# Quantized inner values turned by a DMA, together with another order of loads and set-up

## The chip, the cores and the metric

The kernel runs on one core of a Trainium2 chip. The core has TensorE (PE: matrix products and transposes, results in PSUM), VectorE (DVE), ScalarE (ACT), GpSimd (POOL), SyncE (SP, which only issues DMAs and waits) and 16 DMA engines. Every engine takes its own instructions in order; between engines there are only semaphores. The metric is the device time of one execution in microseconds (us).

## The reference

There are 8 sequences of 512 tokens with 256 channels. Each one goes through these steps:

```python
y = x @ W[subject].T + b[subject]              # a weight chosen by the batch's id
q, k, v = silu(y@Wq), silu(y@Wk), y@Wv         # 16 heads of 16 channels
q, k = [t*cos, t*sin]                          # positions, 32 channels a head
out = (tril(q @ k.T) @ v) @ Wo * sigmoid(y@G1@G2)
x = x + layernorm(out)
# cond2: a recurrent mixing of x
ctx = ema(x);  wg = sigmoid([x, ctx] @ Wg.T + bg);  gated = x*wg
mod = 0.5 + sigmoid(gelu(x@Wn1.T + bn1) @ Wn2.T + bn2)      # 8 traces
traces_d = ema_d(gated * mod_d)                # 8 decays, one for each trace
temporal = sum_d softmax(blend)_d * traces_d
c = layernorm((gelu(x@Wsoma.T + bsoma) * sigmoid(temporal@Wtemp.T + btemp)) @ Wout.T)
# feed-forward with quantized activations (to 127 steps) and weights (-1, 0, 1)
h = silu(quant(c) @ wq(w_gate).T) * (quant(c) @ wq(w_up).T)     # 1024 inner values
x = x + quant(h) @ wq(w_down).T
```

`quant` scales each token's row by its largest absolute value, rounds and scales back; `wq` does so with the mean absolute value of the whole weight.

## The kernel before, in words

A batch is one sequence of 512 tokens, handled as four tiles of 128 tokens. It goes through three generators: `attention(b)`, `cond2(b)` and `ffn(b)`. Two more, `setup_cond2` and `setup_ffn`, prepare constants. A planner at the end of the kernel (from L898) runs them in turn. Each generator issues some instructions, adds their estimated TensorE time to the planner's clock with `spent(work, then)`, and yields the time `then` microseconds on at which its next part is due. Of the parts that are due, the one of the lowest rank goes first: set-up (0), feed-forward (1), cond2 (2), attention (3); if none is due, the clock jumps to the earliest. This makes the program's order. The framework then assigns buffers and semaphores and orders each engine's instructions, where some move ahead of their place in the program. Attention of a batch starts once the one before has issued its second `output`; so in the middle attention(b+2), cond2(b+1) and ffn(b) run beside each other.

The feed-forward works by token tiles. `hidden(t)` (L843) multiplies the turned input `cqT` with `w_gateT` and `w_upT` (L851), takes silu on ScalarE (L854) and the product on VectorE (L855, `h`), finds each row's largest value (`hmax`, L857), and rounds to whole numbers in bf16: `hq`, 128 tokens x 1024 inner values (L861, L863). The product with `w_downT` needs the inner values on the partitions. So TensorE turns `hq` in eight blocks of 128x128 into a PSUM bank (`phq`, L875), ScalarE copies them to `hqT` (L877), and eight matmuls make `pd` (L881). VectorE scales it and adds the residual (`res`, L883), and SyncE writes the tile out (L884). The planner gives the turning 0.6 of TensorE time and makes `pd` due 1.2 later. `hidden(t+1)` is issued before tile t is turned; `h`, `hq`, `hqT` and `res` have two buffers each.

The attention turns its input (`pxT`, L212; ScalarE copies it to `xT`, L213), multiplies by the chosen weight `wt` (`py`, L219), adds `beta_a` to the residual on GpSimd (L222), and then for each token tile projects (`pkq`, `pv`, `sg`), multiplies by cosine and sine on GpSimd (`ktok`, `qtok`, L256), turns (`pkT`, `pqT`) and gathers chunk states (`pst`, `total`, `st`). `energies` and `output` follow, and at the end the gate and the layer norm (`og`, `rstd_a`, L454 to L464). The result is what cond2 turns first (`px2T`, L660). cond2 ends with its layer norm and the quantized `cq` (L795 to L817).

The beginning: SyncE loads the first input, weight and bias. ScalarE issues thirteen loads (L125 to L145 and the rows of `setup_cond2`), GpSimd the others: the weights of cond2, the small vectors, `blend` broadcast to all partitions, and the feed-forward weights, which pass through the two buffers of `h`, so that one weight is loaded after the one before has been quantized (L630). `setup_cond2` computes the softmax of `blend` on all partitions (L600 to L606), spreads its rows to `bw_r` by 16 small DMAs on SyncE (L613), and spreads the decay rates `nsp_d` to `nsp_r` by 8 small DMAs on GpSimd (L585).

Of the kernel before, what the change touches and what calls it, by code (L numbers as in the profile page):

```python
# [8 lines left out]
F32 = mybir.dt.float32  # L9
BF = mybir.dt.bfloat16  # L10
# [8 lines left out]
MAGIC = 12582912.0  # L19

# [10 lines left out]
def adaln_attn_ffn_kernel(ctx: ExitStack, tc: tile.TileContext, a: dict, out: bass.AP):  # L31
# [85 lines left out]
    def load_w(name, src, pool=cp, tag=None, eng=nc.scalar):  # L117
        rows, cols = src.shape
        t = pool.tile([P, rows // P, cols], F32, tag=tag or name, name=name)
        eng.dma_start(t, src.rearrange("(k p) n -> p k n", p=P))  # L120
        return t

    def load_row(name, src):
        t = cp.tile([P, src.shape[0]], F32, name=name)
        nc.scalar.dma_start(t, src.partition_broadcast(P))  # L125
        return t
# [7 lines left out]
    wv = load_w("wv", a["wv"])  # L134
# [4 lines left out]
    nc.scalar.dma_start(g1[:, :, :HD], a["g1"].rearrange("(k p) n -> p k n", p=P))  # L139
    g2 = cp.tile([64, C], F32, name="g2")  # L140
    nc.vector.memset(g2, 0.0)
    for u in range(2):
        nc.scalar.dma_start(g2[32 * u : 32 * u + HD, :], a["g2"])
    gamma_a = load_row("gamma_a", a["gamma_a"])
    beta_a = load_row("beta_a", a["beta_a"])  # L145

# [59 lines left out]
    def attention(b, xs, wt, bt):  # L206
# [14 lines left out]

        nc.gpsimd.tensor_add(xs, xs, beta_a.unsqueeze(1).to_broadcast([P, NT, C]))  # L222
# [179 lines left out]
        turned(3)  # L402
        spent(2.0, 0)
# [67 lines left out]
    w = {}  # L471

    def setup_cond2():

        for n in ("wgT", "wn1T", "wsomaT", "wtempT", "woutT"):
            w[n] = load_w(n, a[n], eng=nc.gpsimd)

        means = p1.tile([P, KC], F32, tag="means", name="means")
        nc.vector.tensor_reduce(means, w["woutT"], AX.X, ALU.add)
        nc.vector.tensor_scalar(means, means, 1.0 / C, None, ALU.mult)  # L480
        for k in range(KC):
            nc.vector.tensor_scalar(w["woutT"][:, k, :], w["woutT"][:, k, :], means[:, k : k + 1], None, ALU.subtract)
        for n in ("bg", "gamma_c", "beta_c"):
            w[n] = load_row(n, a[n])

        w["wn2"] = cp.tile([HN + 1, D], F32, name="wn2")
        nc.gpsimd.dma_start(w["wn2"][:HN, :], a["wn2T"])
        nc.gpsimd.dma_start(w["wn2"][HN : HN + 1, :], a["bn2"].rearrange("(o d) -> o d", o=1))
        w["bn1"] = cp.tile([HN, 1], F32, name="bn1")
        nc.gpsimd.dma_start(w["bn1"], a["bn1"].rearrange("(p o) -> p o", o=1))  # L490
        for n in ("bsoma", "btemp"):
            w[n] = cp.tile([P, KC], F32, name=n)
            nc.gpsimd.dma_start(w[n], a[n])
        yield now[0] + 6.0
        nc.vector.tensor_scalar(w["btemp"], w["btemp"], 0.5, None, ALU.mult)


        tau = p1.tile([P, D + 1], F32, tag="tau", name="tau")
        nc.gpsimd.dma_start(tau, a["taus"].partition_broadcast(P))
        tau_d = p1.tile([D, 1], F32, tag="tau_d", name="tau_d")  # L500
        nc.gpsimd.dma_start(tau_d, a["taus"][:D].rearrange("(p o) -> p o", o=1))
        sps = []
        for t, name in ((tau, "sp"), (tau_d, "sp_d")):
            e = p1.tile(list(t.shape), F32, tag=name + "_e", name=name + "_e")
            nc.vector.scalar_tensor_tensor(e, t, -1.0, t, ALU.mult, ALU.max)
            nc.scalar.activation(e, e, AF.Exp, scale=-1.0)
            sps.append(e)
        for e in sps:
            nc.scalar.activation(e, e, AF.Ln, bias=1.0)
        for t, e in zip((tau, tau_d), sps):  # L510
            nc.vector.scalar_tensor_tensor(e, t, 0.0, e, ALU.max, ALU.add)
        sp, sp_d = sps
# [483 lines left out]
```

## Time and profile before

| What | us |
|---|---|
| Median of 3 runs (lowest to highest) | 832.13 (831.72 to 835.56) |
| Profiled execution, its own time | 831.28 |
| Its span, from the first to the last instruction | 829.5 |
| TensorE busy in the span | 724.8 |
| VectorE busy | 531.7 |
| ScalarE busy | 306.0 |
| GpSimd busy | 239.8 |
| First `px2T` (cond2 of batch 0 starts) | 89.04 |
| Last `res` | 826.19 |

The profile page tells the busy time of each engine (1), the span in 40 slices (2), the DMA queues (3), the chain of waits that ended last (4), the costliest groups of instructions (5) and the DMA issues (6). In a line of the timeline, the first number is the start in us, the second the duration (of all instructions that were merged, if it ends in a count), and the bracket the idle time of the engine just before it, with what ended it. A releaser is inferred. `PEld` is TensorE's weight load, which runs beside `PE`.

### The profile page before, as it was taken

How to read it: one execution, taken by the hardware profiler on the slowest of the kernel's cores; microseconds unless marked ns; L12 is line 12 of the kernel's file. 1: busy time of each engine (PE TensorE's matmuls, PEld its weight loads, DVE VectorE, ACT ScalarE, POOL GpSimd, SP SyncE). 2: the span in 40 equal slices, each digit the busy share in tenths (PEclk: the TensorE clock that was granted, in tenths of full speed). 3: DMA queues.
4: the chain of work that ended last, by engine and by line, in shares of the span. 5: the costliest groups of instructions: out<-in, count | busy, mean ns of one | idle time of the engine just before them, and what ended most of it. 6: DMA issues, size and time to landing. Idle time of an engine off the chain costs nothing.

```text
span 829.5 us, 21857 instructions
## 1 busy us (share of the span) xinstructions
PE 724.8 (87%) x9630; PEld 496.4 (60%) x9630; DVE 531.7 (64%) x1035; ACT 306.0 (37%) x536; POOL 239.8 (29%) x274
## 2 busy tenths in 40 slices
PE   3878899989997999999997999799998998696745
PEld 2557568556773667656873777566774676464423
DVE  5897545767458755784568754776469554775375
ACT  1741432345224432373224432354226421351122
POOL 6770442311502152223522151213403250111000
PEclk8956999989998999999998999999999999897667
DMA  8411000001000010001000010000000000000000
GB/s 265 141 30 55 13 1 4 15 0 31 24 3 13 14 39 3 15 14 40 3 2 13 20 34 4 13 7 21 3 2 8 19 4 3 0 12 15 1 0 26
DMA packets 16849, 19.29 MB, mean 23 GB/s; under 512 B 3331, under 2 KB 15395, under 8 KB 16755
## 3 DMA queue, kind: packets, MB, share of 16 engines
q1 hardware_dynamic: 12418, 10.56, 4.1%
q0 software_dynamic: 2048, 5.58, 2.1%
q10 hardware_dynamic: 2288, 1.76, 0.7%
q8 instruction: 75, 1.23, 0.6%
q14 instruction: 20, 0.16, 0.1%
HBM read 13.63 MB, written 4.19 MB: 21 GB/s over the span
## 4 chain that ended last, share of the span: by engine, by line
PE 64%; DVE 20%; issue 5%; POOL 5%; DMA 3%; ACT 2%; ACTq 0%; POOLq 0%; DVEq 0%
PE ptr L749 9%; PE pwg L699 7%; PE pkq L233 5%; PE pe L313 4%; PE po L335 4%; PE ptg L766 4%; PE pw_gateT L851 3%; PE pso L678 3%; PE pd L881 3%; PE pw_upT L851 3%; PE pv L238 2%; PE pst L276 2%; PE pkT L263 2%; PE pqT L263 2%; PE phq L875 2%
## 5 line engine op out<-in xcount | busy, mean ns | idle before, releaser
L754 DVE SCALAR_TENSOR_TENSOR tempT<-ptr,bw_c,tempT 128x512 f32<-128x512 f32 x128 | 96.0, 750 | 85.6 <-PE ptr L749 83.0
L749 PE MATMUL ptr<-dm,gated 64*128 64x128 f32 x1024 | 82.8, 301 | 10.4 <-DVE tempT L754 10.4
L256 POOL TENSOR_TENSOR ktok<-sg,cs 128x512 f32<-128x512 f32 x32 | 43.6, 1363 | 153.8 <-ACT sg L240 151.7
L749 PEld LDWEIGHTS ptr<-dm,gated 64*128 64x128 f32 x1024 | 69.0, 200 | 29.1 <-issue 20.7
L233 PE MATMUL pkq<-wkq,yT 128*128 128x512 f32 x128 | 64.2, 621 | 0.2 <-ACT kT L264 0.2
L855 DVE SCALAR_TENSOR_TENSOR h<-pw_upT,steps,sig 128x512 f32<-128x512 f32 x64 | 45.8, 744 | 18.6 <-ACT sig L854 10.3
L854 ACT ACTIVATE sig<-pw_gateT,steps 128x512 f32<-128x512 f32 x64 | 42.2, 685 | 26.8 <-PE pw_gateT L851 18.0
L287 POOL TENSOR_TENSOR st<-total,own 128x256 f32<-128x256 f32 x56 | 40.8, 746 | 37.2 <-DVE total L297 37.1
L318 DVE TENSOR_TENSOR et<-pe,causal 128x512 f32<-128x512 f32 x64 | 41.1, 684 | 15.1 <-PE pe L313 15.1
L256 POOL TENSOR_TENSOR qtok<-sg,cs 128x512 f32<-128x512 f32 x32 | 43.6, 1362 | 13.7 <-PE pst L276 13.5
L851 PEld LDWEIGHTS <-cqT 128*128 128x128 bf16 x256 | 28.0, 109 | 31.7 <-issue 11.9
L851 PE MATMUL pw_gateT<-w_gateT,cqT 128*128 128x512 bf16 x128 | 45.2, 433 | 0.0
L313 PE MATMUL pe<-qT,kT 32*64 32x64 f32 x2048 | 43.3, 229 | 0.2 <-ACT sg L240 0.2
L313 PEld LDWEIGHTS pe<-qT,kT 32*64 32x64 f32 x2048 | 37.1, 141 | 9.7 <-issue 7.5
L851 PE MATMUL pw_upT<-w_upT,cqT 128*128 128x512 bf16 x128 | 42.5, 417 | 0.0
L738 POOL TENSOR_TENSOR dm<-decay,mod 128x512 f32<-128x512 f32 x32 | 33.6, 1062 | 27.3 <-PE ptr L749 27.1
L240 ACT ACTIVATE sg<-pkq 128x512 f32<-128x512 f32 x32 | 19.1, 598 | 57.6 <-PE pkq L233 57.5
L877 ACT COPY hqT<-phq 128x1024 bf16<-128x1024 bf16 x32 | 32.4, 1011 | 21.4 <-PE phq L875 21.4
L881 PE MATMUL pd<-w_downT,hqT 128*128 128x256 bf16 x256 | 35.0, 282 | 5.6 <-ACT hqT L877 5.6
L857 DVE TENSOR_REDUCE hmax<-h 128x1 f32<-128x1024 f32 x32 | 38.9, 1217 | 0.6
L219 PE MATMUL py<-xT,wt 128*128 128x512 f32 x64 | 31.3, 629 | 8.1 <-ACT xT L213 8.1
L222 POOL TENSOR_TENSOR x<-x,beta_a 128x1024 f32<-128x1024 f32 x8 | 18.9, 2368 | 66.8 <-PE pxT L212 60.1
(221 smaller groups left out, 1459.1 us busy)
## 6 DMA issues: line engine op xcount, KB each, us to landing
x<-in_x_dram SPq DMA_DIRECT2D x8, 512.0 KB
out_dram<-res SPq DMA_DIRECT2D x32, 128.0 KB
wt<-in_weightT_dram SPq DMA_DIRECT2D x8, 256.0 KB
w_gateT_raw<-in_w_gateT_dram POOLq DMA_DIRECT2D x2, 512.0 KB, 5.1
bw<-in_blend_dram POOLq DMA_DIRECT2D x2, 512.0 KB, 4.8
w_upT_raw<-in_w_upT_dram POOLq DMA_DIRECT2D x2, 512.0 KB, 3.7
w_downT_raw<-in_w_downT_dram POOLq DMA_DIRECT2D x2, 512.0 KB, 4.7
wgT<-in_wgT_dram POOLq DMA_DIRECT2D x1, 512.0 KB, 7.1
```

Of the source, the lines that this page charges most:

```text
L233: nc.tensor.matmul(pkq, yT[:, k, chunk(t)], wkq[:, k].rearrange("p e c -> p (e c)"), start=k == 0, stop=k == KC - 1)
L256: nc.gpsimd.tensor_mul(tok.rearrange("p (h e d) -> p h e d", e=2, d=HD), sgs[t][:, i].unsqueeze(2).to_broadcast([P, H, 2, HD]), cs[:, t, : ...
L287: nc.gpsimd.tensor_mul(sts[c], total[0].rearrange("p (g f) -> p g f", g=NG).unsqueeze(2).to_broadcast([P, NG, 2, 2 * HD]), own.rearrange(" ...
L313: nc.tensor.matmul(pes[e][64 * r : 64 * (r + 1), g, u, :], kT[rows, g, at], qT[rows, g, at], start=True, stop=True)
L318: nc.vector.tensor_mul(et.rearrange("p g u n -> p (g u) n"), pes[e].rearrange("p g u n -> p (g u) n"), causal.unsqueeze(1).to_broadcast([P ...
L699: nc.tensor.matmul(pwg[:, u, :], src[:, k % KC, chunk(t + u)], w["wgT"][:, k, :], start=k == 0, stop=k == 2 * KC - 1,)
L749: nc.tensor.matmul(ptr[:, r, :, t, :], gated[rows, t, chunk(k)], dm[rows, t], start=True, stop=True)
L754: nc.vector.scalar_tensor_tensor(acc, ptr[:, :, e].rearrange("p r t n -> p r (t n)"), w["bw_c"][:, k, d + e : d + e + 1], acc, ALU.mult, A ...
L851: nc.tensor.matmul(pm, cqT[:, k, chunk(t)], w[n][:, k, cols], start=k == 0, stop=k == KC - 1)
L854: nc.scalar.activation(sig, pgu[0], AF.Silu, scale=steps[:, 0, t : t + 1])
L855: nc.vector.scalar_tensor_tensor(h[:, cols], pgu[1], steps[:, 1, t : t + 1], sig, ALU.mult, ALU.mult)
L881: nc.tensor.matmul(pd, hqT[:, chunk(k)], w["w_downT"][:, k, :], start=k == 0, stop=k == KI - 1)
```

## The change

Three things are different.

*The feed-forward's turning.* One DMA with `transpose=True`, issued on SyncE's queue, takes `hq` (128x1024, bf16, in SBUF) to `hqT` (128 partitions x 8 blocks x 128). The eight TensorE transposes, the PSUM bank and ScalarE's copy are gone. The planner counts no TensorE time for it and makes `pd` due 4.0 later.

*Loads.* ScalarE issues four loads (`theta_c`, `wk`, `wq`, `wv`). All others are issued on SyncE at the start, behind the first input, and GpSimd issues none. Both halves of all three feed-forward weights have tiles of their own, which later serve as `h`, `cT`, `gated`, `c2` and `og`. `blend` is loaded once, as 8 rows.

*Set-up and small moves.* The softmax of `blend` is taken on its turned form (128 channels x 2 x 8) and spread by two TensorE transposes; the decay rates are selected by a comparison with each partition's trace number. No DMA is left in the set-up generators. They are due at 12.0 and 18.0 on the planner's clock instead of 5.0 and 5.0. The row means of `woutT` are subtracted at the end of `setup_cond2`. `h1` is a constant tile whose row of ones is written once, not in each batch. The addition of `beta_a` moves from behind `py` to behind `turned(3)`.

```diff
-    def load_w(name, src, pool=cp, tag=None, eng=nc.scalar):
+    def load_w(name, src, eng=nc.sync):
...
-        nc.scalar.dma_start(t, src.partition_broadcast(P))
+        nc.sync.dma_start(t, src.partition_broadcast(P))
...
-    wv = load_w("wv", a["wv"])
+    wv = load_w("wv", a["wv"], eng=nc.scalar)
...
+    tau = p1.tile([P, D + 1], F32, tag="tau", name="tau")
+    nc.sync.dma_start(tau, a["taus"].partition_broadcast(P))
+    blend = p1.tile([D, C], F32, tag="blend", name="blend")
+    nc.sync.dma_start(blend, a["blend"])
+    raws = {}
+
+    def load_raw(n, *places):
+        rows, cols = a[n].shape
+        half = rows // P // 2
+        raws[n] = [
+            pool.tile([P, half * cols], F32, tag=tag, name=f"{n}_raw_{s}") for s, (pool, tag) in enumerate(places)
+        ]
+        for s, raw in enumerate(raws[n]):
+            nc.sync.dma_start(
+                raw.rearrange("p (k n) -> p k n", k=half), a[n].rearrange("(s k p) n -> s p k n", p=P, s=2)[s]
+            )
+
+    load_raw("w_gateT", (p2, "h"), (p2, "h"))
+    for n in ("wgT", "wn1T", "wsomaT"):
+        w[n] = load_w(n, a[n])
+    load_raw("w_upT", (p1, "cT"), (p1, "gated"))
...
+    load_raw("w_downT", (p1, "c2"), (p1, "og"))
+    for n in ("wtempT", "woutT"):
+        w[n] = load_w(n, a[n])
...
             nc.scalar.activation(yT[:, o, :], py, AF.Identity, bias=bt[:, o : o + 1])
-
-        nc.gpsimd.tensor_add(xs, xs, beta_a.unsqueeze(1).to_broadcast([P, NT, C]))
         wt_free[0] = b + 1
...
         output(0)
         turned(3)
+
+        nc.gpsimd.tensor_add(xs, xs, beta_a.unsqueeze(1).to_broadcast([P, NT, C]))
...
+    h1 = cp.tile([HN + 1, T], F32, name="h1")
+    nc.gpsimd.memset(h1[HN : HN + 1, :], 1.0)
...
-        nsp_r = p1.tile([P, 1], F32, tag="nsp_r", name="nsp_r")
-        nc.vector.memset(nsp_r, 0.0)
-        for t in range(NT):
-            for r in range(2):
-                q = 32 * t + D * r
-                nc.gpsimd.dma_start(nsp_r[q : q + D, :], nsp_d)
+        nc.vector.tensor_mul(own_trace, own_trace, nsp[:, :D])
+        nsp_r = p1.tile([P, 1], F32, tag="nsp_r", name="nsp_r")
+        nc.vector.tensor_reduce(nsp_r, own_trace, AX.X, ALU.add)
...
-            bw = p1.tile([P, D, P], F32, tag=("gated", "c2")[k], name=f"bw_{k}")
-            nc.gpsimd.dma_start(bw, a["blend"][:, chunk(k)].partition_broadcast(P))
...
-            for t in range(NT):
-                for r in range(2):
-                    q = 32 * t + D * r
-                    nc.sync.dma_start(w["bw_r"][q : q + D, chunk(k)], bw[0:1])
+            nc.tensor.transpose(ptb[:, chunk(k)], many[:, k].rearrange("p m d -> p (m d)"), ident)
+        nc.vector.tensor_copy(w["bw_r"], ptb[:, :C])
...
-            for s in range(2):
-                raw = p2.tile([P, half * cols], F32, tag="h", name=f"{n}_raw_{s}")
-                nc.gpsimd.dma_start(raw.rearrange("p (k n) -> p k n", k=half), src[s])
+            for s, raw in enumerate(raws[n]):
                 nc.vector.tensor_reduce(sums[:, s : s + 1], raw, AX.X, ALU.add, apply_absolute_value=True)
...
-            pt = bank(f"phq_{b}_{t}", BF)
-            for k in range(KI):
-                nc.tensor.transpose(pt[:, chunk(k)], hq[:, chunk(k)], ident_bf)
-            hqT = p2.tile([P, INNER], BF, tag="hqT", name=f"hqT_{b}_{t}")
-            nc.scalar.copy(hqT, pt)
-            yield spent(0.6, 1.2)
+            hqT = p2.tile([P, KI, P], BF, tag="hqT", name=f"hqT_{b}_{t}")
+            nc.sync.dma_start(hqT, hq, transpose=True)
+            yield spent(0.0, 4.0)
             pd = bank(f"pd_{b}_{t}")[:, :C]
             for k in range(KI):
-                nc.tensor.matmul(pd, hqT[:, chunk(k)], w["w_downT"][:, k, :], start=k == 0, stop=k == KI - 1)
+                nc.tensor.matmul(pd, hqT[:, k, :], w["w_downT"][:, k, :], start=k == 0, stop=k == KI - 1)
...
-    start((0, 0), 0, "setup_cond2", setup_cond2(), 5.0)
-    start((0, 1), 0, "setup_ffn", setup_ffn(), 5.0)
+    start((0, 0), 0, "setup_cond2", setup_cond2(), 12.0)
+    start((0, 1), 0, "setup_ffn", setup_ffn(), 18.0)
```

## The prediction

> **What bounds the kernel now.** I read the first page for the engines, the chain that ended last for who carries the end, the table of stretches for where TensorE stands still, and then the timeline and the groups of the places that the change touches. On the page, TensorE is the busiest engine and has most of the chain:
>
> ```profile
> PE 724.8 (87%) x9630; PEld 496.4 (60%) x9630; DVE 531.7 (64%) x1035; ACT 306.0 (37%) x536; POOL 239.8 (29%) x274
> ...
> PE 64%; DVE 20%; issue 5%; POOL 5%; DMA 3%; ACT 2%; ACTq 0%; POOLq 0%; DVEq 0%
> ```
>
> The stretches (microseconds, then busy time of PE, PEld, DVE, ACT, POOL, the granted clock, DMA share, GB/s) tell the stages apart:
>
> ```profile
> 40.00:60.00 20.00, 12.37 (x235) 10.11 (x242) 18.12 (x20) 8.76 (x15) 16.34 (x20) 0.59 0.15 48
> 60.00:89.00 29.00, 25.44 (x501) 19.11 (x489) 22.02 (x46) 5.68 (x12) 6.07 (x6) 0.69 0.14 40
> ...
> 168.50:260.00 91.50, 84.20 (x1197) 58.35 (x1195) 57.59 (x115) 35.07 (x62) 23.05 (x26) 0.97 0.06 16
> ...
> 783.00:829.50 46.50, 25.31 (x120) 13.55 (x120) 26.86 (x58) 13.31 (x23) 1.80 (x4) 0.73 0.03 11
> ```
>
> A batch in the middle takes 91.5 us with 84.2 of TensorE. Until 89 us only the first attention and the set-up run, TensorE waits a lot, and its clock is 0.59 to 0.69. From 783 us on only the last feed-forward is left, and its chain of waits counts.
>
> The beginning, in order of time:
>
> ```profile
> 13.86 0.54 ACTq L125 DMA_DIRECT2D beta_c<-in_beta_c_dram  x1
> ...
> 16.36 5.38 PE L219 MATMUL py<-xT,wt 128*128 128x512 f32 x8 [7.35 <-ACT xT L213]
> ...
> 38.94 3.85 POOL L585 DMA_DIRECT2D nsp_r<-nsp_d  x7 [0.38 <-DVE nsp_d L516]
> ...
> 47.63 1.12 PE L263 MATMUL pkT<-ident,ktok 128*128 128x128 f32 x4 [8.16 <-DVE red L604]
> ```
>
> ScalarE issues loads until 14.40 and so copies the turned input only from 15.72, though TensorE had turned it by 9.00. TensorE then idles 8.16 us before 47.63: the ktok that it waits for is queued on GpSimd behind the nsp_r copies, the decay product and w_upT.
>
> The part that is exchanged, by groups (busy, mean ns of one, idle before and its releaser):
>
> ```profile
> L877 ACT COPY hqT<-phq 128x1024 bf16<-128x1024 bf16 x32 | 32.4, 1011 | 21.4 <-PE phq L875 21.4
> ...
> L881 PE MATMUL pd<-w_downT,hqT 128*128 128x256 bf16 x256 | 35.0, 282 | 5.6 <-ACT hqT L877 5.6
> ...
> L875 PE MATMUL phq<-ident_bf,hq 128*128 128x128 bf16 x256 | 20.5, 225 | 12.6 <-DVE hmax L824 6.0 <-DVE hq L863 5.5 <-DVE res L883 0.8
> ```
>
> One turn costs TensorE 20.5/32 = 0.64 us busy and ScalarE 1.01 us.
>
> **The change part by part.** The sum is made against the profiled execution: span 829.5, its own time 831.3 us, which is 0.85 under the median of 832.13.
>
> *Loads and set-up.* ScalarE issues four loads in place of thirteen (the last, wv, ends at 2.82), so the input's copies follow the turning at 9.00 and py starts near 10.1, not 16.36: 6.3 us off the path, if wt has landed (wv, issued nearby, landed at 9.42). GpSimd loses twenty DMA issues of 0.55 to 1.3 us and the eight nsp_r copies (4.4 us); VectorE loses the blend's broadcast arithmetic (L600 3.8, L601 2.8, L603 3.8, L604 1.9, L605 0.5, L606 3.4: 16.2 us), for which come small instructions of 0.15 to 0.2 us each, about 5 us together. Of the 8.16 us stall I take 6 away. The feed-forward weights, all in their own tiles, no longer wait for one another (GpSimd waited 8.3 us for w_upT's quantizing before it loaded w_downT, and TensorE 2.0 us at 75.44 for w_downT's sums); with the second half of the blend gone from VectorE I put the stalls between 56 and 76 us at 4.7 less. Together 17.0. The lower bound is 6.3, if the rest comes back as VectorE work in another order. The upper is 25: py at 10, some 45 us for one attention's TensorE work (busy time of its groups, an eighth each: 43.6), and 9 for the layer norm behind it give 64 instead of 89. What moves to SyncE is 27 issues of 0.4 to 0.6 us, ahead of the second batch's input; 6.8 MB at the 265 GB/s of the first slice are 26 us, and that input is read only at 82.9, which covers it. If they came late, VectorE would stand in front of them, as it did 6.1 us for woutT at 20.35.
>
> *The addition of beta_a.* It is 2.35 us of GpSimd, today at the seam of two batches:
>
> ```profile
> 250.59 2.35 POOL L222 TENSOR_TENSOR x<-x,beta_a 128x1024 f32<-128x1024 f32 x1
> 250.90 0.16 DVE L826 RECIPROCAL c_inv<-amax 128x2 f32<-128x2 f32 x1
> 250.98 1.98 DVE L808 TENSOR_TENSOR steps<-amax,wstep 128x4 f32<-128x4 f32 x1
> ```
>
> L808 has a median of 0.143 us; here it lasted until the addition was over. At the six seams some VectorE instruction is stretched so: by 1.5, 1.8, 1.2, 1.5, 1.8 and 0.7 us, 8.5 together, in front of cq or the next batch's px2T, for which TensorE waits. After turned(3) there is other TensorE work, and GpSimd is 25% busy; I credit 7 and keep 0 to 8.5.
>
> *h1's memset.* 0.52 us on GpSimd a batch, with 15.1 us idle before it and nobody waiting: nothing. If GpSimd were full it would be 0.5 a batch.
>
> *The turns off TensorE and ScalarE.* In seven feed-forwards (28 turns) other stages run beside them: 28 x 0.64 = 17.9 us of TensorE work. Of that I take the chain's TensorE share, 64%: 11.5. The bounds are 0 (VectorE sets the feed-forward's pace) and 17.9. ScalarE's 1.01 us copies lie beside TensorE's work; what TensorE waited for them (5.6) goes.
>
> *The turn by DMA.* No row shows one. Its time L, from hq to hqT in place: lowest, SyncE's issue of an SBUF-to-SBUF copy (bw_r, 0.62 us) and the landing of the tiny nsp_r copies (1.7): 2.3. Highest, eight 128x128 blocks one after another at the pace of the bw_r issues (17.71/16 = 1.11 each) and that landing: 10.6. Nearest is a transfer of the same 256 KB:
>
> ```profile
> woutT<-in_woutT_dram POOLq DMA_DIRECT2D x1, 256.0 KB, 3.1
> ```
>
> wtempT took 3.2; so 3.2 + 0.6 = 3.8 us. The planner now puts pd 4.0 us of other work behind the turn, where copy and turn had 1.8. With hq on time, 3.8 is covered. Where hq is late (TensorE stood 12.6 us for it at phq), the wait moves on to pd: no change. Without that cover each us of L costs 28 us. On SyncE a turn waits for hq, and behind it wait the outputs; ahead of it is the output of the tile before, which waits for res. SyncE stood 426 us waiting for res, so the 32 issues (20 us) are hidden, as are later inputs, which are loaded a batch ahead.
>
> The Trainium skill speaks against this step: "VectorE: DVE Perf Modes", sections "The three transpose paths" and "Rules for kernel authors", gives 1309 ns for a 128x128 bf16 block by DMA against 390 ns by TensorE, and advises TensorE when PSUM will do. By that page, block after block, L would be 10.5, an estimate, and the sum about 1,010 us. The same skill, "Advanced Engine Details and Errata", section "X-Bar Transpose (TRN2)", calls such DMAs as fast as ordinary ones, which would leave the sum as it is. No run so far shows either.
>
> *The last feed-forward* has nothing beside it. From hq to hqT it took 805.84 to 807.99 and, at the end, 822.0 to 824.2: 2.2 us; now 3.8, so 1.6 more at the last tile. Before it, turn t+1 on SyncE stands behind output t, so it starts 0.5 us after res(t) at the earliest, and res(t) is itself later: I add 3.4 over three tiles. Together 5 (bounds 1 and 4 x 8.4 = 34 at L = 10.6).
>
> Sum: 831.3 - 17.0 - 7.0 - 11.5 + 5.0 = 800.8, and 0.85 more to stand against the median: 802.
>
> **The rivals.**
> *The turn is too slow, and pd's wait takes the place of phq's.* TensorE takes its work in order, so every us beyond 4.0 stops it 28 times and the tail four times. The gains less the tail are 30.5, used up at L = 4.9. At 5.5 the time is 802 + 42 + 7 = 851; with eight blocks in a row (8.9) 802 + 137 + 20 = 959. For it speak that no row shows such a DMA and that hq is often late; against it the 3.1 for 256 KB. Chance 0.22, of which 0.09 is the block-after-block case, the one of the skill's first page.
> *TensorE does less, but the period stays*, set by VectorE's 57.6 us and the seams: 802 + 11.5 = 813. *The beginning gives only ScalarE's 6.3 us*: 802 + 10.7 = 813 too. Chance of one of them 0.18; both, 824, 0.06.
> *More than forecast*: L near 2.3, so that TensorE also loses part of the 12.6 us, and 25 at the beginning: 786. Chance 0.10.
> *Gains and a turn slightly over 4.9 cancel*: within 0.5% (828 to 836, about what a measurement of this kernel can tell from no change). Chance 0.06.
>
> **How the numbers follow.** My forecast, 795 to 808, has 0.38. Faster: 0.38 + 0.18 + 0.06 + 0.10 = 0.72; same 0.06; slower 0.22. The range leaves out about 0.07 below 785 and 0.12 above 862 (L of 5.9).
>
> **What would show it.** py near 10 us; the first px2T near 72, not 89; no 8 us TensorE stall at 40 to 48; L808 at 0.14 throughout. phq and its copy gone; pd's idle time in the middle not above some 18 us (now 12.6 + 5.6 with phq's); hq to pd in the last feed-forward 3.8 us. If pd idles 30 us or more, L is over 5 and the first rival is right; if px2T begins after 82, the beginning is mis-sized.

## The result, and the profile after

The changed kernel takes 809.15 us (median of 4 runs, 804.65 to 811.26) against 831.99 (831.72 to 835.56) before: a ratio of 0.9715 with a 95% interval of 0.9678 to 0.9752, so 21 to 27 us less. The profiled execution is the slowest of the four: its own time is 811.26 us, its span 809.6, and before had 831.28 and 829.5.

The first `px2T` of each batch cuts the span into comparable pieces. (The start of batch 1's is used, because from there on the seams of all batches look alike.)

| Piece, us | before | after | difference |
|---|---|---|---|
| start to batch 0's first `px2T` | 89.04 | 80.67 | -8.4 |
| start to batch 1's first `px2T` | 168.53 | 164.03 | -4.5 |
| from there to batch 7's, six batches | 552.0 | 537.1 | -14.9 |
| from there to the end | 109.0 | 108.5 | -0.5 |
| span | 829.5 | 809.6 | -19.9 |

From the page of after, the busy time of the engines, the chain that ended last, the group of `pd`, the group of `pcq`, and the DMA issue of the turn:

```profile
PE 696.3 (86%) x9362; PEld 473.7 (59%) x9362; DVE 517.7 (64%) x1031; ACT 269.7 (33%) x496; POOL 218.4 (27%) x238
...
PE 60%; DVE 13%; issue 3%; POOL 3%; DMA 2%; ACT 0%; POOLq 0%; DVEq 0%; ACTq 0%; SPq 0%
...
L877 PE MATMUL pd<-w_downT,hqT 128*128 128x256 bf16 x256 | 36.6, 291 | 15.9 <-DMA hqT<-hq 14.9
...
L835 PE MATMUL pcq<-ident_bf,cq 128*128 128x128 bf16 x64 | 8.2, 270 | 36.7 <-DVE cq L816 36.7
...
hqT<-hq SPq DMA_TRANSPOSE x32, 3.1
```

TensorE lost 28.5 us of work and ScalarE 36.3. The turn lands 3.1 us after its issue. `phq` is gone with its 12.6 us of idle time, and `pd` idles 15.9 in place of 5.6. `pcq`, the turning of cond2's quantized result, idles 36.7 instead of 25.3: more of TensorE's time at the seam of two batches is spent waiting for VectorE's `cq`.

TensorE's waits in the six batches in the middle (line, releaser, us in total, times, longest) tell where; first before, then after:

```profile
PE pcq L836 <- DVE cq L817: 16.0, 8, 5.7
...
PE px2T L660 <- DVE x L464: 3.8, 2, 1.9
...
PE px2T L660 <- DVE h L855: 1.7, 1, 1.7
```

```profile
PE pcq L835 <- DVE cq L816: 27.5, 12, 5.7
...
PE pd L877 <- DMA hqT<-hq: 0.2, 1, 0.2
```

So `pcq` has the longest wait there in both. With `px2T`, which directly follows it at the seam and no longer waits in after, the seams cost 21.5 us of waiting before and 27.5 after.

The waits only change places, though: the 6.2 us in front of `phq` and the 5.5 in front of `px2T` are gone, `pcq` has 11.5 more, and in all TensorE stands idle for 40.4 us of these six batches before and 41.1 after. What became less is its busy time, from 511.6 to 496.0 us.

`pd` waits 0.2 us there for the DMA in 24 turns. Most of its wait is in the last feed-forward, as its timeline shows:

```profile
784.37 3.01 SPq L873 DMA_TRANSPOSE hqT<-hq  x2
...
787.45 1.89 PE L877 MATMUL pd<-w_downT,hqT 128*128 128x256 bf16 x8 [6.81 <-DMA hqT<-hq]
...
799.65 3.00 SPq L873 DMA_TRANSPOSE hqT<-hq  x2
...
802.78 3.66 PE L877 MATMUL pd<-w_downT,hqT 128*128 128x256 bf16 x16 [7.09 <-DMA hqT<-hq]
```

The framework issues two turns behind each other (`x2`), so the last feed-forward has two such waits and not four. From the end of `hq` (799.58) to `pd` it is 3.2 us.

The beginning went otherwise than forecast. The stretches of after (columns as in the prediction):

```profile
40.00:60.00 20.00, 17.15 (x593) 13.78 (x592) 18.61 (x33) 9.41 (x22) 10.57 (x9) 1.00 0.02 4
60.00:80.70 20.70, 10.55 (x179) 7.51 (x179) 10.17 (x25) 3.10 (x6) 3.76 (x3) 0.90 0.06 15
164.00:252.70 88.70, 83.69 (x1172) 57.54 (x1170) 60.42 (x117) 31.94 (x59) 26.12 (x27) 0.96 0.12 28
```

Between 40 and 60 us TensorE now works 17.15 us of 20 (12.37 before), at a granted clock of 1.00 instead of 0.59: the stall of 8.16 us is gone. But from 60 us to the first `px2T` it works only half of the time. The timeline of that beginning in after:

```profile
14.19 0.38 PE L566 MATMUL pt_bw<-ident,blend 8*128 8x8 f32 x2 [5.97 <-DMA blend<-in_blend_dram]
...
15.77 0.21 ACT L577 ACTIVATE nsp<-nsp 128x9 f32<-128x9 f32 x1 [11.69 <-DVE nsp L576]
...
17.41 1.06 ACT L254 COPY xT<-pxT 128x512 f32<-128x512 f32 x2
...
69.24 0.16 DVE L641 TENSOR_SCALAR wstep<-pwsum 128x1 f32<-128x1 f32 x1 [9.10 <-PE pwsum L638]
...
69.63 2.87 DVE L647 TENSOR_SCALAR w_downT_raw<-w_downT_raw,winv 128x1024 f32<-128x1024 f32 x2
...
75.01 0.76 DVE L495 SCALAR_TENSOR_TENSOR og<-gate,pw 128x256 f32<-128x256 f32 x2
...
80.67 1.21 PE L661 MATMUL px2T<-ident,x 128*128 128x128 f32 x4 [7.87 <-DVE x L505]
```

ScalarE's copy of the turned input stands behind the softplus of the decay rates (`nsp`), which waits for a small load (`tau`) queued behind `x`, `wt` and others on SyncE. `py` starts at 18.02, later than before's 16.36. At the other end, VectorE stands 9.10 us for the weight sums of `w_downT`, quantizes it from 69.63 on, and only then starts `og`. (VectorE had summed the raw weights up by 45.0, but TensorE adds these sums up, `pwsum`, only at 68.70, behind `pw` and `pxT`.) A reason can be seen in the code: the second half of `w_downT`'s raw values lies in the buffer that `og` takes next.

### The profile page after: what moved, and what is told of

It is laid out like the page before. It is cut to its first block, busy times and chain, and to the rows that moved or that the text cites. A ratio compares the mean times of both kernels' runs of the same rounds, so it can differ in the third digit from the quotient of the medians.

```text
span 809.6 us, 21287 instructions
## 1 busy us (share of the span) xinstructions
PE 696.3 (86%) x9362; PEld 473.7 (59%) x9362; DVE 517.7 (64%) x1031; ACT 269.7 (33%) x496; POOL 218.4 (27%) x238
## 3 DMA queue, kind: packets, MB, share of 16 engines
q1 hardware_dynamic: 51140, 24.40, 12.5%
## 4 chain that ended last, share of the span: by engine, by line
PE 60%; DVE 13%; issue 3%; POOL 3%; DMA 2%; ACT 0%; POOLq 0%; DVEq 0%; ACTq 0%; SPq 0%
PE ptr L748 8%; PE pwg L698 6%; PE pw_gateT L850 4%; PE pd L877 4%; PE po L374 4%; PE pw_upT L850 4%; PE pe L352 3%; PE pso L677 3%; PE ptg L765 3%; PE pw L490 3%; PE pkq L272 3%; DVE c L800 2%; DMA hqT<-hq 2%; PE pst L315 2%; PE pqT L302 2%
## 5 line engine op out<-in xcount | busy, mean ns | idle before, releaser
L748 PE MATMUL ptr<-dm,gated 64*128 64x128 f32 x1024 | 79.8, 299 | 10.4 <-DVE tempT L753 10.4
L748 PEld LDWEIGHTS ptr<-dm,gated 64*128 64x128 f32 x1024 | 67.2, 200 | 25.2 <-issue 20.6
L272 PE MATMUL pkq<-wkq,yT 128*128 128x512 f32 x128 | 66.1, 634 | 0.0
L854 DVE SCALAR_TENSOR_TENSOR h<-pw_upT,steps,sig 128x512 f32<-128x512 f32 x64 | 46.1, 742 | 17.6 <-ACT sig L853 11.1
L326 POOL TENSOR_TENSOR st<-total,own 128x256 f32<-128x256 f32 x56 | 41.7, 762 | 41.1 <-DVE total L336 41.1
L877 PE MATMUL pd<-w_downT,hqT 128*128 128x256 bf16 x256 | 36.6, 291 | 15.9 <-DMA hqT<-hq 14.9
L357 DVE TENSOR_TENSOR et<-pe,causal 128x512 f32<-128x512 f32 x64 | 41.1, 684 | 13.2 <-PE pe L352 13.2
L850 PE MATMUL pw_upT<-w_upT,cqT 128*128 128x512 bf16 x128 | 44.7, 436 | 0.0
L877 PEld LDWEIGHTS <-hqT 128*128 128x128 bf16 x256 | 25.7, 104 | 27.2 <-DMA hqT<-hq 20.2
L352 PE MATMUL pe<-qT,kT 32*64 32x64 f32 x2048 | 40.1, 220 | 1.0 <-DVE et L357 1.0
L835 PE MATMUL pcq<-ident_bf,cq 128*128 128x128 bf16 x64 | 8.2, 270 | 36.7 <-DVE cq L816 36.7
L352 PEld LDWEIGHTS pe<-qT,kT 32*64 32x64 f32 x2048 | 34.4, 133 | 9.1 <-issue 7.1
L374 PE MATMUL po<-et,vz 64*32 64x64 f32 x2048 | 27.5, 225 | 14.1 <-issue 12.6
```

The lines of the kernel that those rows point to most:

```text
L272: nc.tensor.matmul(pkq, yT[:, k, chunk(t)], wkq[:, k].rearrange("p e c -> p (e c)"), start=k == 0, stop=k == KC - 1)
L326: nc.gpsimd.tensor_mul(sts[c], total[0].rearrange("p (g f) -> p g f", g=NG).unsqueeze(2).to_broadcast([P, NG, 2, 2 * HD]), own.rearrange(" ...
L352: nc.tensor.matmul(pes[e][64 * r : 64 * (r + 1), g, u, :], kT[rows, g, at], qT[rows, g, at], start=True, stop=True)
L374: nc.tensor.matmul(po[r][q : q + 32, half, u, :], *factors, start=(r, q) not in begun, stop=last)
L748: nc.tensor.matmul(ptr[:, r, :, t, :], gated[rows, t, chunk(k)], dm[rows, t], start=True, stop=True)
L850: nc.tensor.matmul(pm, cqT[:, k, chunk(t)], w[n][:, k, cols], start=k == 0, stop=k == KC - 1)
```

## The experiments

Each kernel is one edit of the changed kernel, unless it says otherwise. The table has them all; ratios are to runs of the kernel before beside them, and the pieces are those of the table above, each from one profile (before: 168.5, 552.0, 109.0). The kernel before had medians of 830.47 beside the first four kernels, 836.25 beside "w_downT elsewhere", "both of these", "no addition" and "turned twice", and 833.82 beside the others, so the ratios compare better than the times.

| Kernel | us, median (range) | ratio [95%] | to batch 1 | six batches | rest |
|---|---|---|---|---|---|
| after, again | 808.09 (803.51 to 809.70) | 0.9721 [0.9687, 0.9755] | 162.1 | 536.5 | 108.6 |
| turn on TensorE | 823.34 (821.07 to 830.79) | 0.9942 [0.9909, 0.9974] | 162.3 | 549.5 | 107.4 |
| DMA turn alone | 815.40 (812.97 to 817.16) | 0.9813 [0.9782, 0.9844] | 169.0 | 538.7 | 106.7 |
| tau first | 806.63 (803.71 to 815.71) | 0.9732 [0.9683, 0.9781] | 162.4 | 536.4 | 107.1 |
| w_downT elsewhere | 803.62 (800.56 to 806.76) | 0.9630 [0.9559, 0.9701] | 155.6 | 535.5 | 107.8 |
| both of these | 805.54 (802.77 to 807.35) | 0.9630 [0.9568, 0.9692] | 160.0 | 537.3 | 108.4 |
| no addition | 794.75 (792.24 to 797.62) | 0.9522 [0.9455, 0.9589] | 161.1 | 521.7 | 107.9 |
| addition later | 798.30 (793.36 to 800.76) | 0.9561 [0.9526, 0.9595] | 164.4 | 525.5 | 107.7 |
| turned twice | 848.41 (845.85 to 851.88) | 1.0156 [1.0085, 1.0227] | 163.1 | 565.1 | 118.9 |
| eight blocks | 996.78 (993.44 to 1003.11) | 1.1944 [1.1902, 1.1985] | 166.2 | 675.7 | 159.5 |
| pd due at once | 889.12 (885.34 to 890.91) | 1.0673 [1.0636, 1.0710] | 165.0 | 598.6 | 120.1 |
| best parts together | 792.66 (784.87 to 793.93) | 0.9487 [0.9449, 0.9526] | 155.7 | 528.5 | 106.7 |

### Which part of the change gives how much

The kernel once more, as the base of the others:

> The changed kernel once more, beside the others on the same chip. 804 to 811 us, as in its four runs; the middle six batches take 537 us between the first turnings of their x2, TensorE idles 7.9 us before the first px2T, and pd waits for the turn by DMA almost only in the last feed-forward.

Measured: 808.09. The beginning varies by 2 us between the two profiles (164.0 and 162.1 to batch 1), the six batches by 0.6.

The new beginning with the old turning:

```diff
-            hqT = p2.tile([P, KI, P], BF, tag="hqT", name=f"hqT_{b}_{t}")
-            nc.sync.dma_start(hqT, hq, transpose=True)
-            yield spent(0.0, 4.0)
+            pt = bank(f"phq_{b}_{t}", BF)
+            for k in range(KI):
+                nc.tensor.transpose(pt[:, chunk(k)], hq[:, chunk(k)], ident_bf)
+            hqT = p2.tile([P, INNER], BF, tag="hqT", name=f"hqT_{b}_{t}")
+            nc.scalar.copy(hqT, pt)
+            yield spent(0.6, 1.2)
...
```

> The new loads and set-up alone: the turn is back on TensorE and ScalarE with its old due times. Theory (the turn's 0.64 us of TensorE work a tile is what shortened the middle by 14.9 us; the new beginning gave only 4.5): about 825 us, the middle six batches again near 550. Rival A (the middle became shorter by the other moves, the turn is worth nothing): 809, middle near 537. Rival B (the new beginning is worth the predicted 17 and the turn loses): below 805.

Measured: 823.34, a ratio of 0.9942, which is 4.8 us less than before (2 to 8). To batch 1 it is as fast as after (162.3), the six batches take 549.5, 13.0 more than the 536.5 of "after, again", and the rest 107.4, 1.2 less.

The reverse, the old beginning with the DMA, its 4.0 and the new form of `hqT` put into the kernel before:

```diff
-            pt = bank(f"phq_{b}_{t}", BF)
...
-            yield spent(0.6, 1.2)
...
+            nc.sync.dma_start(hqT, hq, transpose=True)
+            yield spent(0.0, 4.0)
...
```

> The turn by DMA alone, in the kernel before with its old loads and set-up. Theory: 832 - 15 in the middle and -0.5 at the end, 816 to 818 us, with the first px2T still at 89. Rival A (the turn is worth nothing without the new set-up): 830 to 833. Rival B (only what was predicted, 11.5 less 5 of the end): 825.

Measured: 815.40, a ratio of 0.9813: 15.5 us less than before (13 to 18), 13.3 of them in the six batches. The two ratios multiplied give 0.976 against the 0.972 of both together: the parts add up. The turning by DMA carries two thirds to four fifths of the gain (15.5 of 23.2 us here, 18.4 by what is missing without it). In both comparisons the six batches show the same as above: TensorE stands idle for 40.3 us with its own turning and 40.4 in "after, again", for 40.4 in before and 39.9 with the DMA turn alone, while its busy time falls by 13.1 and by 12.8 us.

### What the beginning still waits for

`tau` and `blend` ahead of the large weights, on ScalarE's queue:

```diff
     # right behind theta_c's load
...
+    nc.scalar.dma_start(tau, a["taus"].partition_broadcast(P))
...
+    nc.scalar.dma_start(blend, a["blend"])
...
-    nc.sync.dma_start(tau, a["taus"].partition_broadcast(P))
...
-    nc.sync.dma_start(blend, a["blend"])
```

> In the changed kernel the loads of tau and blend go to ScalarE's queue right behind theta_c, ahead of wk, wq and wv. Theory (ScalarE's copy of the turned input stood behind the softplus of tau, which landed at 15.0 us; so py began at 18.0): py begins at 10 to 12, and the first px2T comes 5 to 7 us earlier, at 74 to 76; the time falls by 5 to 7 against the changed kernel. Rival (VectorE's og waits for the quantizing of w_downT, whose raw half lies in og's buffer, and this sets the end of the first attention): py earlier, px2T at 78 to 80, and the time less than 2 us lower.

Measured: `py` starts at 14.38 and not 18.02, but batch 0's first `px2T` gets no earlier: it comes at 81.02, after the same 7.87 us. That is nearer to the rival than to the theory. In this kernel's timeline VectorE stands behind `w_downT` as in after:

```profile
69.36 0.16 DVE L641 TENSOR_SCALAR wstep<-pwsum 128x1 f32<-128x1 f32 x1 [7.66 <-PE pwsum L638]
```

The other suspect is the buffer. The second half of `w_downT` goes into the tile that later serves as `soma`, which cond2 of batch 0 needs only behind `px2T`:

```diff
-    load_raw("w_downT", (p1, "c2"), (p1, "og"))
...
     # behind the second activation that makes the cosines
+    load_raw("w_downT", (p1, "c2"), (p1, "soma"))
```

> In the changed kernel the second raw half of w_downT lies in soma's buffer, not in og's, and w_downT is loaded last (behind the cosines, which hold soma until then). Theory (og could not be written before w_downT's second half was quantized, and this sets the end of the first attention): og starts with pw, VectorE's 7.7 us wait for pwsum ahead of it is gone, TensorE's 7.9 us before the first px2T go to about 1, px2T at 73 to 75 and the time 6 to 7 us under the changed kernel: 801 to 802. Rival (the quantizing is only postponed and stops something else, or the later loads come too late): px2T earlier, but the second px2T still at 162, no gain.

Measured: 803.62 us, a ratio of 0.963 against 0.972. In its timeline `og` runs first, and `w_downT` behind it:

```profile
65.84 0.75 DVE L496 SCALAR_TENSOR_TENSOR og<-gate,pw 128x256 f32<-128x256 f32 x2 [1.60 <-PE pw L491]
...
74.35 0.15 DVE L642 TENSOR_SCALAR wstep<-pwsum 128x1 f32<-128x1 f32 x1
```

```profile
73.30 1.12 PE L662 MATMUL px2T<-ident,x 128*128 128x128 f32 x3 [1.03 <-DVE x L506]
```

`px2T` starts 7.4 us earlier than in after, and its 7.87 us of waiting are down to 1.6 in two waits. At batch 1, 6.5 us of it are kept (155.6 against 162.1). So the shared buffer set the end of the first attention, and `tau` did not. (The edit also loads `w_downT` later, but VectorE takes its sums at the same time in both kernels, from 42.6 and 42.7 us on, so the load is not what lets `og` run first.) The two ratios alone do not show the gain, since their intervals overlap; it is read from the pieces, and the kernel with the best parts has it again (155.7).

Both edits at once:

> Both mends of the beginning: tau and blend loaded first, and w_downT's half out of og's buffer. Theory: with og free the 3.5 us by which py came earlier in e3_tau_first now reach the end of the first attention: px2T at 70 to 71, 9 to 10 us under the changed kernel, 798 to 799. Rival (the middle of the first attention waits for VectorE's set-up work, so an earlier py is worth nothing): like e4_down_elsewhere.

Measured: 805.54, and `px2T` at 77.23, 3.9 us later than with the second edit alone, though `py` starts at 13.72. Its ratio is the same, 0.963. With `tau` early, VectorE has its set-up work and the projections' work together. The stretches of this kernel, then of "w_downT elsewhere":

```profile
20.00:30.00 10.00, 5.39 (x29) 3.51 (x31) 10.00 (x29) 9.62 (x13) 3.74 (x3) 0.91 0.70 191
30.00:40.00 10.00, 10.00 (x98) 6.29 (x95) 9.20 (x17) 6.76 (x14) 8.79 (x8) 0.75 0.67 211
40.00:50.00 10.00, 5.77 (x164) 5.00 (x164) 9.93 (x14) 4.30 (x8) 7.97 (x7) 0.77 0.01 2
```

```profile
20.00:30.00 10.00, 8.74 (x23) 4.04 (x21) 9.42 (x28) 7.20 (x10) 0.39 (x1) 0.93 0.68 201
30.00:40.00 10.00, 8.77 (x100) 6.12 (x101) 7.32 (x13) 7.57 (x14) 9.53 (x11) 0.83 0.75 235
40.00:50.00 10.00, 8.29 (x233) 6.60 (x238) 7.39 (x13) 5.88 (x15) 7.72 (x8) 1.00 0.02 4
```

VectorE's column (the third with an x) has 29.1 us of 30 in the first, 24.1 in the second. In the first kernel TensorE then waits 3.8 us for VectorE's `et` (0.9 in the second), and its clock is 0.77 from 40 to 50 us instead of 1.00. An earlier start of `py` is used up there. That VectorE is what uses it up is read from these lines; no run took VectorE's set-up work away.

### What the addition of beta_a costs

The change puts it behind `turned(3)` in the program, but the framework issues it where its inputs are ready. At a seam of after, GpSimd's and VectorE's timelines:

```profile
237.12 0.75 DVE L495 SCALAR_TENSOR_TENSOR og<-gate,pw 128x256 f32<-128x256 f32 x2 [0.32 <-PE pw L490]
...
238.04 2.36 POOL L443 TENSOR_TENSOR x<-x,beta_a 128x1024 f32<-128x1024 f32 x1 [17.73 <-PE pxT L253]
...
238.67 2.41 DVE L502 SCALAR_TENSOR_TENSOR og<-og,mv,gamma_a 128x256 f32<-128x256 f32 x2
...
240.36 0.42 POOL L242 TENSOR_SCALAR rstd_a<-mv 128x4 f32<-128x4 f32 x1
```

The addition waits for `pxT` alone and starts at the seam as before. The `og` instruction beside it lasts until the addition is over, and GpSimd's own `rstd_a`, which the residual needs, stands behind the addition. The first experiment leaves the addition out, so this kernel does not compute all of the reference; the remark on beta in its expectation does not hold for the inputs of the runs, where the row is not zero.

```diff
-        nc.gpsimd.tensor_add(xs, xs, beta_a.unsqueeze(1).to_broadcast([P, NT, C]))
```

> The changed kernel without the addition of beta_a to the residual (this input's beta is zero; the work is left out, eight additions of 2.35 us on GpSimd). Theory (the addition's cost at the seam is real, but the move did not take it away, since it still runs there: it stretched L502 from 0.86 to 2.4 us): 6 to 10 us under the changed kernel, 798 to 802, and pcq's idle time of 36.7 us falls by as much. Rival (the stretched instructions are not on the path): 806 to 809, pcq's idle time unchanged.

Measured: 794.75 us, a ratio of 0.952 against 0.972. The six batches take 521.7 us, 14.8 less than in "after, again" (536.5), more than was expected. `pcq`'s wait there falls by less than that, from 27.4 to 22.6.

The second keeps it, and ties it behind the last `qtok` of the attention, so that it can't go to the seam:

```diff
-            nc.gpsimd.tensor_mul(
+            last[0] = nc.gpsimd.tensor_mul(
...
-        nc.gpsimd.tensor_add(xs, xs, beta_a.unsqueeze(1).to_broadcast([P, NT, C]))
+        with tc.issue_after(last[0].ins):
+            nc.gpsimd.tensor_add(xs, xs, beta_a.unsqueeze(1).to_broadcast([P, NT, C]))
```

> In the changed kernel the addition of beta_a is tied behind the last qtok of its attention on GpSimd, so that it cannot be taken ahead to the seam. Theory (the addition at the seam holds VectorE's L502 and the rstd_a behind it for 2.35 us, and e6_no_add gained 14.8 us in the middle by leaving it out): most of that, 10 to 15 us under the changed kernel, 793 to 798, with L502 back at 0.86 for two. Rival (it stretches a tempT or delays st or dm in its new place as much): 804 to 809.

Measured: 798.30, a ratio of 0.956. The six batches take 525.5, 11.0 less than in "after, again". The addition still takes 2.4 us, in the middle of the attention, where nobody waits for it. The seam of this kernel, answering to the lines above:

```profile
236.12 0.75 DVE L497 SCALAR_TENSOR_TENSOR og<-gate,pw 128x256 f32<-128x256 f32 x2 [0.31 <-PE pw L492]
...
237.66 0.47 DVE L504 SCALAR_TENSOR_TENSOR og<-og,mv,gamma_a 128x256 f32<-128x256 f32 x1
237.84 0.39 POOL L242 TENSOR_SCALAR rstd_a<-mv 128x4 f32<-128x4 f32 x1 [18.55 <-DVE mv L237]
```

From the start of `og` to `rstd_a` it is 1.7 us; in after it is 3.2. Only 4.8 of the 11.0 us are less waiting in front of `pcq` (27.4 to 22.6). TensorE's busy time in the six batches falls by 6.2 us (496.1 to 489.9) with the same instructions, and it falls right behind the seams: `pcq`, `px2T` and the products with `w_gateT` and `w_upT` take 6.0 us less. There the granted clock is higher. In the 9.35 us behind the five seams of the six batches that hold an addition in after, it is 0.78 on average in after and 0.86 here; at the seam shown it is 0.74 and 1.00. The stretched VectorE groups, before, then after, then with the addition later (busy us, mean ns):

```profile
L461 DVE SCALAR_TENSOR_TENSOR og<-og,mv,gamma_a 128x256 f32<-128x256 f32 x32 | 21.1, 681 | 0.0
L801 DVE SCALAR_TENSOR_TENSOR c<-c,rstd,beta_c 128x256 f32<-128x256 f32 x32 | 16.7, 544 | 2.2 <-POOL rstd L799 1.8
L808 DVE TENSOR_TENSOR steps<-amax,wstep 128x4 f32<-128x4 f32 x16 | 6.0, 373 | 0.0
```

```profile
L502 DVE SCALAR_TENSOR_TENSOR og<-og,mv,gamma_a 128x256 f32<-128x256 f32 x32 | 23.2, 761 | 0.0
L800 DVE SCALAR_TENSOR_TENSOR c<-c,rstd,beta_c 128x256 f32<-128x256 f32 x32 | 20.8, 671 | 1.1 <-POOL rstd L798 0.4
L807 DVE TENSOR_TENSOR steps<-amax,wstep 128x4 f32<-128x4 f32 x16 | 2.3, 143 | 0.0
```

```profile
L504 DVE SCALAR_TENSOR_TENSOR og<-og,mv,gamma_a 128x256 f32<-128x256 f32 x32 | 14.4, 472 | 0.0
L802 DVE SCALAR_TENSOR_TENSOR c<-c,rstd,beta_c 128x256 f32<-128x256 f32 x32 | 14.7, 479 | 1.1 <-POOL rstd L800 0.4
L809 DVE TENSOR_TENSOR steps<-amax,wstep 128x4 f32<-128x4 f32 x16 | 8.1, 506 | 0.0
```

Together 43.8, 46.3 and 37.2 us. `steps` alone would have said that the move worked (6.0 to 2.3); the addition only stretches `og` instead, once in each of six batches of after. Not all of the sums is the addition's: the long `c` of after (six of 1.50 us) lie beside `ktok`, and the long `steps` of the last kernel (six of 1.11) beside `qtok`. All three have two inputs in SBUF. The Trainium skill, "SBUF — State Buffer", section "Who interferes with whom", says that a VectorE instruction with two SBUF inputs contends with a GpSimd instruction that reads SBUF, and that the order of issue decides which of two such instructions is blocked. The trace agrees: `og` took 2.0 us at most in after and 0.48 at most where the addition lies elsewhere.

### What the turn's time costs

Every turn issued twice into the same buffer, the second behind the first's landing, so that a turn takes some 6.2 us:

```diff
             nc.sync.dma_start(hqT, hq, transpose=True)
+            nc.sync.dma_start(hqT, hq, transpose=True)
```

> Every turn is made twice, one after the other into the same buffer, so that L goes from 3.1 to about 6.2 us. By the prediction's slope (28 us for each us beyond 4.0, and four times the excess at the end) 28 x 2.2 + 4 x 3.1 = 74 us more than the changed kernel: 880, with pd idle some 60 us in the middle. Rival (the order of TensorE's work leaves far more than 4.0 us between a turn and its pd, so only the last feed-forward sees it): two pairs of turns, 6 to 7 us each way at most, 812 to 816, pd's idle time in the middle under 5 us.

Measured: 848.41, some 40 us more than "after, again" (its span is 847.1 against 807.2; by the ratios 36). The six batches grew by 28.6 us and the rest by 10.3. In the six batches TensorE waited for it in 12 places:

```profile
PE pd L878 <- DMA hqT<-hq: 22.4, 12, 3.2
```

The turn now takes 2.2 us more than the planner's 4.0. Over 24 turns that would be 53 us; it was 28.6, of which 22 are TensorE's idle time, and 12 of the 24 turns made nobody wait. The planner's 4.0 is not what the trace shows as cover: in the first feed-forward of after, `pd` follows the issue of its turn by 5.2, 9.5, 3.1 and 5.4 us, so the third turn, which takes 3.1, has nothing to spare.

Eight DMAs of one 128x128 block each in place of one:

```diff
-            nc.sync.dma_start(hqT, hq, transpose=True)
+            for k in range(KI):
+                nc.sync.dma_start(hqT[:, k, :], hq[:, chunk(k)], transpose=True)
```

> Each tile is turned by eight DMAs of 128x128 in place of one. If SyncE takes for each what it takes for a whole tile (1.23 us), the last block lands 8.6 + 3.1 = 11.7 us after hq, 8.6 us more than with one DMA. By the slope of e7_twice in the middle (28.6 us for 3.1 us of L) and more, because the slack is used up by then: at least 80 and at most 28 x 7.7 + 4 x 8.6 = 250 us more, 890 to 1060. Rival (a small turn is issued in 0.3 us or less): L about 5.5, 820 to 835. The landing of one 128x128 block is to be seen as well; the Trainium skill, VectorE: DVE Perf Modes, section The three transpose paths, gives 1309 ns for it.

Measured: 996.78. From its page, the group of `pd` and the issues:

```profile
L878 PE MATMUL pd<-w_downT,hqT 128*128 128x256 bf16 x256 | 64.8, 310 | 134.0 <-DMA hqT<-hq 133.8
...
hqT<-hq SPq DMA_TRANSPOSE x256, 2.4
```

One issue takes SyncE 1.230 us (median), for a block of 32 KB as for the whole tile of 256 KB (1.232 in after). Eight blocks so need 7 x 1.23 + 2.4 = 11.0 us (11.1 to 12.5 in the trace), the whole tile 3.1. This is the block-after-block case of the first rival. It forecast 959 for 8.9 us; its slope gives 1,027 for 11.0, so it said about what the case costs.

The cover taken away, the turn left as it is:

```diff
-            yield spent(0.0, 4.0)
+            yield spent(0.0, 0.0)
```

> The planner makes pd due at once behind the turn, not 4.0 later. If that due time is what covers the turn, about half of the 28 turns in the middle wait some 3 us on TensorE: 30 to 45 us more than the changed kernel, 840 to 855. Rival (the framework orders TensorE's work by its own estimate of the DMA and needs no due time): 804 to 812.

Measured: 889.12, some 80 us more than "after, again", about twice what was expected. TensorE's longest waits in the six batches (62 us longer):

```profile
PE pcq L835 <- DVE cq L816: 26.9, 11, 5.7
PE ptr L748 <- DVE gated L708: 20.7, 6, 3.6
PE pd L877 <- DMA hqT<-hq: 17.6, 12, 3.0
```

17.6 us of it are `pd`'s own wait. Another 20.7 are cond2's `ptr` behind `gated`, which does not appear among after's waits. Together TensorE is idle for 36.4 us more; the other 25.7 of the 62 are its busy time, 521.8 against 496.1 us for the same instructions, at a granted clock of 0.92 against 0.96. So the planner's 4.0 is what hides the turn, and pulling `pd` ahead disturbs the order of the other stages too. Why `gated` comes so late then was not taken apart.

### The best parts together

Addition later, `w_downT` elsewhere, and TensorE's turning kept for the last feed-forward, where nothing covers a DMA:

```diff
-            hqT = p2.tile([P, KI, P], BF, tag="hqT", name=f"hqT_{b}_{t}")
-            nc.sync.dma_start(hqT, hq, transpose=True)
-            yield spent(0.0, 4.0)
+            if b < B - 1:
...
+                yield spent(0.0, 4.0)
+            else:
...
+                yield spent(0.6, 1.2)
```

> The changed kernel with three mends: the addition tied behind qtok as in e9_add_after, w_downT's half out of og's buffer as in e4_down_elsewhere, and the last feed-forward alone turned by TensorE and ScalarE, where nothing covers a DMA. If the gains add: 10 to 15, 7 and 1 us under the changed kernel, 785 to 790. If the seam and the beginning share a limit: 793 to 800.

Measured: 792.66, a ratio of 0.9487 [0.9449, 0.9526]: 5.1% under the kernel before. The piece to batch 1 keeps the 6.4 us of `w_downT` (155.7), the rest is at 106.7 (108.6 in "after, again"), and the six batches gain 8.0 of the 11.0. So the time lies between the two forecasts: the gains add in part.

## Why the prediction was right, and where not

The forecast of 802, with a range of 785 to 862, was in the right direction and 7 us under the 809. Its terms did less well than its sum: two were too large, one was too small, and the cost at the end hardly came. That these errors partly cancel, and the sum comes so near, is luck.

*Loads and set-up, -17.0: measured -4.5 to -6.5.* The three parts fared differently. The stall of 8.16 us at 47 went, as stepped out. "Py starts near 10.1" failed: the step looked at ScalarE's DMA issues and not at what else is queued ahead of the copy. The softplus of `tau` stands there and waits for a load that the change put behind large ones on SyncE. Even so, this step was worth nothing: "6.3 us off the path" took `py` for the path, and with `py` at 14.38 `px2T` came no earlier. "The feed-forward weights, all in their own tiles, no longer wait for one another" was true and missed the other side, that somebody waits for these tiles: `og` had to wait for the quantizing of `w_downT`. With that undone the beginning gives 12.9 us (155.6 against 168.5), nearer to the 17. The working had the buffers' later names from the change's diff in front of it (`(p1, "og")`), so this wait could have been read there.

*The addition of beta_a, -7.0: about nothing.* (With TensorE's turn the six batches took 549.5 against 552.0, and that holds all that the other parts do there.) The stretching was read rightly from the trace, but for one seam: `og` there lasts 2.09 us against 0.47, 1.6 more and not 1.2, so the six add up to 9.1 and not 8.5. Its worth was put too low, at 7: it is 11.0 us in six batches where the addition is really moved, 4.8 of them waits and the rest TensorE's work behind the seams. But the step took a place in the program for a place in time. The trace of before already had the hint: the addition, too, started when `pxT` was done. In the changed kernel it waits for nothing more than that.

*The turns off TensorE, -11.5: measured -13 in the six batches, 15 in all.* The term was mis-sized. The chain's share of TensorE, 64%, was taken for the part of its lost work that would come off the time. In the six batches of before, TensorE spent 14.7 us on `phq`, and 13.0 and 13.3 came off in the two pairs of runs, nearly all of it, since TensorE's idle time stayed at 40 us. That it stays was foreseen, but not where: the working let `phq`'s waits "move on to `pd`", and with 4.0 of cover `hqT` was there in time. They came back in front of `pcq` (16.0 to 27.5). That less TensorE work ahead of `cq` is what lengthened `pcq`'s wait is argued from this sum; no run shows it alone.

*The turn's time, 3.8: measured 3.2* from `hq` to `pd` (3.1 from issue to landing). The row taken, a plain transfer of 256 KB, was the right one; the 0.6 added for the issue was counted twice, since the landing is timed from the issue. The Trainium skill's "Advanced Engine Details and Errata", section "X-Bar Transpose (TRN2)", agrees: 3.1 us, against 3.1 and 3.2 us for the plain 256 KB loads. The Trainium skill's page that spoke against the change, "VectorE: DVE Perf Modes", section "The three transpose paths", gives 1309 ns for a block by DMA. The blocks of the kernel with eight DMAs came at 1.23 us each, near that figure, and one alone landed 2.4 us after its issue; a tile that is issued whole does not take eight times as long.

*The last feed-forward, +5: measured -0.5, between -2.2 and +1.2.* The longer waits did come (6.8 and 7.1 us of waiting), but two turns share one wait, so "four times" was wrong. Against the TensorE turning with the same beginning it costs 1.2 us (108.6 against 107.4); in the old beginning it is 2.2 less than before (106.7 against 109.0). It is at the edge of what two profiles tell apart.

*The first rival's slope, 28 us for each us of L, "used up at L = 4.9".* It overstated the slope: from 3.8 to 6.2 it gives 28 x 2.2 = 62 us and 4 x 2.4 = 10 at the end, 71 together; turning twice cost 40, of which 28.6 in the six batches. The rest grew by 10.3, of which 6.4 are the two waits of the last feed-forward (6.81 and 7.09 became 10.07 and 10.23) and others belong to the seventh; the middle grew by half of what was said, since 12 of 24 turns made nobody wait. The rival's direction was right: at 6.2 the kernel is slower than before. And the far end (eight blocks) is about as expensive as the rival said, which is in part luck: its pace of 1.11 us a block was read from the 17.71 us of 16 `bw_r` issues, and 7 us of these were spent waiting for the second `bw`. The issues themselves follow each other by 0.66 us. A turning DMA takes SyncE 1.23.

*What was to show it.* `py` at 10: no. The first `px2T` near 72, "after 82 the beginning is mis-sized": 80.7, short of that mark, and mis-sized all the same. The 8 us stall: gone. L808 at 0.14: yes, and it proved nothing. `pd`'s idle time in the middle not above 18: 1.2 us in the six batches.

## What to carry to other kernels

Ask of every buffer that a set-up step borrows who takes it next and when: a load that waits for nobody can make the main path wait, and taking another buffer gave 6.5 us of the beginning here. A line moved in the program need not move in time; look in the trace for what the instruction waits for, and tie it where it is to stay. A transposing DMA that is issued once for a whole tile, with enough other TensorE work put in front of its reader, takes TensorE's transposes and ScalarE's copies off almost for nothing, and without that cover this kernel is slower than the one that had them (889 against 834).

## What the runs showed of the hardware

A transposing DMA from SBUF to SBUF holds SyncE for 1.23 us at its issue, whether it moves 32 KB or 256 KB, against 0.33 us for an output of 128 KB; it lands 2.4 and 3.1 us after the issue. So the number of DMAs, not their size, was the price. It also makes many packets: with the same loads, the queue's count is 17,348 where TensorE turns and 51,140 with the DMA (1,056 a turn), and its share of the DMA engines 6.2% and 12.5%, while an output lands after 1.7 us in both. An addition of 2.36 us on GpSimd cost some 11 us in six batches, 2.2 for each of the five that lie at their seams, because the layer norm of the attention on VectorE and GpSimd's own next instruction both stood behind it. Less than half of that was TensorE's waiting (4.8 us); the rest was its work behind the wait, 6.2 us longer at a lower granted clock (0.78 against 0.86 behind these seams).
